# A routed feed-forward layer: the address of a tile's down weights found inside the next tile's up products, and the last 128 tokens handled some tiles later

## The chip, the cores and the metric

The kernel runs on one core of one Trainium2 chip. The metric is device time in microseconds (us) of one launch. The kernel before takes 870.91 us, the median of three runs (870.66 to 870.98). The compiler, the inputs and the launch are the same for both kernels.

## What is computed

A cross-attention layer is followed by a gated feed-forward layer with one shared expert and eight routed experts, of which each of the 2048 rows ("tokens": 8 batches of 256 rows, 512 numbers in each) takes two.

```python
x = x + xattn(layernorm(x), ctx, mask, ...)       # 8 batches, 16 heads
flat = layernorm(x).reshape(2048, 512)
shared = (sigmoid(flat @ shared_gate.T) * (flat @ shared_up.T)) @ shared_down.T
top_w, top_idx = top_k(softmax(flat @ router_w.T), 2)          # of 8 experts
ge, ue = einsum("nh,eih->nei", bf16(flat), w_gate), einsum(..., w_up)   # I = 352
de = einsum("nei,ehi->neh", sigmoid(ge) * ue, w_down)
out = layernorm(x) + x + shared + sum over experts of comb * de         # x: after attention
```

(The reference applies the layer to the normalised rows and adds the residual; the comment gives the sum in words.)

## The kernel before, in words

The program is written out by hand: every engine runs its instructions in the order in which the code issues them, and semaphores are put in from the reads and writes of tiles.

**Attention.** The loop over `b`, `g` and `h` (lines 1184 to 1262) runs the 8 batches. Beside it, the feed-forward work of the batch before is woven in by lists of steps: normalising rows (`token_norm`, line 530), turning them so that the hidden dimension lies on partitions (`turn_tokens`, line 547), choosing experts (`route`, line 564), and the shared expert (`shared_units`, line 928). Normalised rows are written to DRAM in `xs`, sorted by expert. Of the last batch, the first 128 rows are done in the loop; the last 128 rows are not sorted, and follow after it.

**Routed experts.** There are 37 tiles (`NT`) of 128 sorted rows, then 8 more tiles (`E`) in which the last 128 rows go through each of the 8 experts in turn. Which expert a sorted tile belongs to is known only at run time. Eight expert numbers are packed as base-8 digits of one integer, and TensorE's sequencer holds the integers in registers (`EIGHT`, line 797). `weights_of` (line 799) takes a tile's digit by a division and a remainder, multiplies it by the size of an expert's weights, and keeps the outcome in a register, `FIRST[t, per]`: once for a tile's gate and up weights (`GU`), once for its down weights (`DN`). It does so when it is first asked for a product's operand. The matmul's moving operand is then addressed by that register plus a constant.

**The order of the stage.** `stream` (line 858) lists the steps, and a round is named here by its tile number t. Round t holds `gate_up_of(t)`: eight products of 352 columns (four into `eg`, four into `eu`, line 820), then on ScalarE a tanh of `eg` (line 825), on VectorE the product `hz` (line 826), and on SyncE the fetch of tile t+3 (line 762). Then comes `down_of(t-2)`: three products of 512 columns into `ey` (line 849), a weighted copy by ScalarE (line 855), and a scatter to DRAM by GpSimd (line 856, recorded at line 195). Then `turn_h(t-1)`: three transposes of `hz` into `pht` (line 834) and their copy to `hT` (`evacuate`, line 95), which VectorE (line 98) and ScalarE (line 100) do in turn. The copy of an even tile is VectorE's, of an odd tile ScalarE's. So `down_of(t-2)` waits for ScalarE's copy in an odd round, for VectorE's in an even one.

**PSUM.** `bank` (line 80) gives out six banks in a ring; two of its six places draw on a pair of buffers with the tag "mm". A round takes four banks: `eg`, `eu`, `ey`, `pht`. `turn_tokens` (`pst`, line 552) and the router's products (`psr`, line 574) take an "mm" buffer directly, without a turn of the ring.

**Rounds and the last 128 tokens.** The code after the attention loop (lines 1264 to 1314) runs rounds 0 and 1, `token_norm` of the last 128 tokens on VectorE, round 2, `turn_tokens`, then rounds 3 to 37, with one of nine steps of `short` after each round from the fourth: eight of `route`, in which the router's products come first, and `weighted`, which makes eight diagonal matrices (line 873). None of these steps issues a DMA. Every third round one row block of the earlier result is read back (`again`, line 905, on GpSimd's queue). The turned rows `xTb`, the diagonals and `xT` are used from tile 37 on and by the shared expert that follows it.

Of the kernel before, what the change touches and what calls it, by code (L numbers as in the profile page):

```python
# [18 lines left out]
B, C, T = 8, 256, 512  # L19
HEADS, HD = 16, 16  # L20
E, I = 8, 352
NKC = T // P
# [10 lines left out]
NT = 2 * NS + E - 1  # L33
# [3 lines left out]
def xattn_ffn_kernel(  # L37
# [20 lines left out]
    nc = tc.nc  # L58
# [21 lines left out]
    def bank(shape, dt, name, own=False):  # L80


        ring.rotate(-1)
        i = 0 if own else ring[-1]
        if i == 0:
            return ps_m.tile(shape, dt, tag="long", name=name, bufs=1)
        if i in (3, 4):
            return ps_s.tile(shape, dt, tag=f"s{i - 2}", name=name)
        if i == 5:
            return ps_av.tile(shape, dt, tag="av", name=name)  # L90
        return ps_m.tile(shape, dt, tag="mm", name=name)
# [438 lines left out]
    def token_norm(b, tt, engine=nc.gpsimd):  # L530
        s = S[b]
        acc = s["acc", tt]
        mv, rs = s.pop(("tstats", tt))
        xn = one.tile([P, T], F32, tag="rd", name="xn")
        engine.tensor_scalar(xn, acc, mv[:, 0:1], rs, ALU.subtract, ALU.mult)
        engine.tensor_add(acc, acc, xn)
        s["xn", tt] = xn
# [3 lines left out]
    def late(tag, n=4):  # L541

        if tag not in LATE:
            LATE[tag] = one.tile([P, n, T], BF16, tag=tag, name="late_" + tag)
        return LATE[tag]

    def turn_tokens(b, tt):
        s = S[b]
        xn = s.pop(("xn", tt))
        if tt == 0:  # L550
            s["xT"] = two.tile([P, NKC, C], F32, tag="xT", name=f"xT{b}")
        ps = ps_m.tile([P, NKC, P], F32, tag="mm", name="pst")
        for kc in range(NKC):
            nc.tensor.transpose(ps[:, kc, :], xn[:, kc * P : (kc + 1) * P], ident)
        cols = slice(tt * P, (tt + 1) * P)
        nc.scalar.copy(s["xT"][:, :, cols], ps)
        if (b, tt) == (B - 1, 1):
            s["xTb"] = late("xm")[:, 0, :].rearrange("p (k n) -> p k n", n=P)
            nc.vector.tensor_copy(s["xTb"], ps)
        else:  # L560
            s["xnb", tt] = three.tile([P, T], BF16, tag="xnb", name="xnb")
            (nc.vector if b == B - 1 else nc.gpsimd).tensor_copy(s["xnb", tt], xn)
# [184 lines left out]
    def expert_tiles():  # L747
# [3 lines left out]
        ROW, EIGHT = [], []  # L751

        def fetch(t):

            if t >= NT:
                return
            if t == 0:
                ROW.extend(numbers(M["row"], THIRDS, mybir.EngineType.SP, P**3 - 1))
            v = ROW[t // 3]
            row = (v // P ** (t % 3)) % P * P if t % 3 else v % P * P  # L760
            XT[t] = late("ctx")[:, t % 4, :].rearrange("p (k n) -> p k n", n=P)
            nc.sync.dma_start_transpose(out=XT[t], in_=xs[bass.ds(row, P), :])
# [21 lines left out]
        GU, DN = (2 * NKC * I, flat(guT)), (3 * T, flat(dT))  # L784
        FIRST = {}
# [13 lines left out]
        def weights_of(t, W, n, at):  # L799


            per, cols = W
            if t >= NT:
                at += (t - NT) * per
                return cols[:, at : at + n]
            if (t, per) not in FIRST:
                v, i = EIGHT[t // 8], t % 8
                first = nc.tensor.to_reg(((v // 8**i) % 8 if i else v % 8) * per)
                FIRST[t, per] = nc.tensor.snap(
                    first, min_val=0, max_val=(E - 1) * per, guaranteed_mod_val=0, out_of_modulus=per  # L810
                )
            return cols[:, bass.ds(FIRST[t, per] + at, n)]

        def gate_up_of(t):
            xT = XT.pop(t) if t < NT else S[B - 1]["xTb"]
            pg = bank([P, I], F32, "eg")
            pu = bank([P, I], F32, "eu")
            for m, ps in ((0, pg), (1, pu)):
                for kc in range(NKC):
                    nc.tensor.matmul(  # L820
                        ps, xT[:, kc, :], weights_of(t, GU, I, (m * NKC + kc) * I),
                        start=(kc == 0), stop=(kc == NKC - 1),
                    )
            th = two.tile([P, I], F32, tag="th", name="eth")
            nc.scalar.activation(th, pg, AF.Tanh, scale=0.5)  # L825
            nc.vector.scalar_tensor_tensor(HZ[t % 2], th, 1.0, pu, ALU.add, ALU.mult)  # L826
            fetch(t + AHEAD)
# [15 lines left out]
        def down_of(t):  # L843
            ht = HT.pop(t)
            if t == NT:
                M["sum"] = bank([P, T], F32, "sum", True)
            ps = bank([P, T], F32, "ey") if t < NT else M["sum"]
            for ic in range(3):
                nc.tensor.matmul(  # L849
                    ps, ht[:, ic, :], weights_of(t, DN, T, ic * T),  # L850
                    start=(t <= NT and ic == 0), stop=(t < NT and ic == 2),
                )
            if t < NT:
                y = (late("mb", 2)[:, t % 5, :] if t % 5 < 2 else late("xm")[:, t % 5 - 1, :])
                nc.scalar.activation(y, ps, AF.Copy, scale=M["weight"][:, t : t + 1])
                scatter(zs, M["to"][:, t : t + 1], y, bounds_check=2 * ROWS - 1, oob_is_err=False)
# [21 lines left out]
    def give_back():  # L878


        halves = [(b, tt) for b in range(B) for tt in range(2)][:NS]
        room = deque(
            [four.tile([P, T], F32, tag=tag, name="again") for tag in "qk" for _ in range(3)]
        )
        for _ in range(3):
            e = three.tile([P, 2, T], F32, tag="e", name="again2")
            room.extend(e[:, i, :] for i in range(2))
        byrow = zs.rearrange("(r c) t -> r c t", c=2)
        Z = []

        def rooms(pool, tag, n, tiles=1):

            for _ in range(tiles):
                z = pool.tile([P, n, 2, T], BF16, tag=tag, name="z_" + tag)
                Z.extend(z[:, j] for j in range(n))

        def all_rooms():
            rooms(two, "V", 3, 2)
            rooms(three, "extra", 1, 3)
            rooms(two, "xT", 2)  # L900
            rooms(two, "x", 2)
            rooms(five, "acc", 1)
            rooms(one, "O", 1)

        def again(b, tt):
            S[b]["acc", tt] = a = room.popleft()
            nc.gpsimd.dma_start(out=a, in_=ACC[b][tt])

        def results(n):
            if not Z:  # L910
                all_rooms()
            nc.sync.dma_start(out=Z[n], in_=byrow[n * P : (n + 1) * P])

        def add(n, c):
            b, tt = halves[n]
            a = S[b]["acc", tt]
            nc.vector.tensor_add(a, a, Z[n][:, c, :])
            if c == 1:
                nc.sync.dma_start(out=out[b, tt * P : (tt + 1) * P, :], in_=a)

        n = range(NS)
        return (
            deque(lambda of=of: again(*of) for of in halves[: 2 * (NB - 1)]),
            deque(lambda i=i: results(i) for i in n), deque(lambda i=i, c=c: add(i, c) for i in n[:-1] for c in range(2)),
            lambda c: Z[NS - 1][:, c, :],
        )
# [257 lines left out]
    for b in range(B):  # L1184
# [10 lines left out]
        if 0 < b:  # L1195
            short = route(b - 1)
# [3 lines left out]
        elif b == B - 1:  # L1200
# [5 lines left out]
            fetch, whom, experts, weighted, tiles = expert_tiles()  # L1206
# [4 lines left out]
        for g in range(NG):  # L1211
            G = NG * b + g
            for h in range(8):
                st, half = divmod(h, 2)

                short = G == 0 and h < 6
# [49 lines left out]
    def some(todo, n):  # L1266
        for _ in range(min(n, len(todo))):
            todo.popleft()[1]()
# [10 lines left out]
    some(units, 3)  # L1279
    some(tiles, 3)  # L1280
    M["whom"]()
    token_norm(B - 1, 1, nc.vector)
    some(tiles, 3)
    turn_tokens(B - 1, 1)
    short = deque(route(B - 1, (1,)) + [(0.0, weighted)])
    again, results, adds, own_results = give_back()
    n = 2
    while n <= NT:
        some(tiles, 3)
        n += 1  # L1290
        if n >= 4:
            some(short, 1)
        if n % 3 == 0 and again:
            again.popleft()()
# [53 lines left out]
```

## Time and profile before

One profiled execution took 869.63 us: a span of 867.8 us from the first to the last instruction, and 1.83 us around it. The clock granted to TensorE was 1.00 throughout.

| what | value |
|---|---|
| median of three runs | 870.91 us |
| the profiled execution, its span | 869.63 us, 867.8 us |
| TensorE matmul busy in the span | 826.3 us (95%) |
| VectorE, ScalarE, GpSimd busy | 67%, 42%, 36% |
| rounds 0 to 4 of the expert stage | from 749.01 to 761.22 us |
| rounds 5 to 36 | from 761.22 to about 832.8 us |
| what follows, to the end | about 35 us |

Busy times are those of the engines proper; "PEld" is TensorE's weight load, which overlaps with its matmuls ("PE"). A name with a q behind it (PEldq) is an instruction of an engine's sequencer, such as the register arithmetic `FUSED_REGOPS`, and isn't counted as busy. In a row of a timeline the first two numbers are start and length in us, and a bracket gives idle time of the engine before it and what ended it. "issue" is time in which the engine waited for nothing that the profile shows. Matmuls are pipelined: a product of 352 columns is recorded with 0.31 us, but the next starts 0.149 us later; for one of 512 columns it is 0.38 us and 0.215 us.

### The profile page before, as it was taken

The numbers are of one execution on the slowest core, as the hardware profiler recorded it, in microseconds if no ns is written. First come the engines' busy times: TensorE is split into PE (matmuls) and PEld (weight loads), VectorE is DVE, ScalarE is ACT, GpSimd is POOL, SyncE is SP. The second block draws the span as 40 slices with busy tenths as digits, with TensorE's granted clock in tenths as the row PEclk, the third lists the DMA queues.
The fourth block names the chain that finished last, engine by engine and source line by source line (L and its number), as shares of the span: only waits on it lengthen the run. The fifth ranks groups of instructions, "written<-read, shape, count | busy, mean of one in ns | idle before, by whom it ended". The sixth has DMA issues, their size and how long they took to land.

```text
span 867.8 us, 13410 instructions
## 1 busy us (share of the span) xinstructions
PE 826.3 (95%) x4987; PEld 340.0 (39%) x4987; DVE 580.8 (67%) x1106; ACT 365.6 (42%) x478; POOL 312.6 (36%) x380
## 2 busy tenths in 40 slices
PE   7988989999999999999999999999999989899997
PEld 4322323333333334333433343433343333455573
DVE  7666767776777677867676778676766674543347
ACT  4234444343344334433443343434343445256632
POOL 3114303543354345343525151605251223155520
PEclk9999999999999999999999999999999999999999
DMA  4107962231551257115712350011000000267556
GB/s 159 46 33 239 342 192 78 34 45 43 128 100 30 41 123 122 23 36 123 128 22 42 90 99 1 26 34 52 1 25 13 13 13 25 61 147 170 150 169 242
DMA packets 91973, 75.05 MB, mean 86 GB/s; under 512 B 60321, under 2 KB 77756, under 8 KB 91526
## 3 DMA queue, kind: packets, MB, share of 16 engines
q1 hardware_dynamic: 85302, 53.84, 22.8%
q0 software_dynamic: 5904, 19.70, 10.8%
q8 instruction: 40, 0.66, 0.3%
q10 hardware_dynamic: 704, 0.66, 0.2%
q14 instruction: 23, 0.19, 0.1%
HBM read 37.84 MB, written 40.79 MB: 91 GB/s over the span
## 4 chain that ended last, share of the span: by engine, by line
PE 74%; DVE 19%; issue 3%; POOL 2%; ACT 1%; DMA 0%; DVEq 0%; ACTq 0%; POOLq 0%
PE s L436 24%; DVE nm L438 10%; PE av L474 9%; PE psy L998 5%; PE pu L940 4%; PE psq L411 3%; PE psk L411 3%; PE ey L849 3%; PE eu L820 3%; PE eg L820 3%; PE pgu L940 3%; PE pg L940 3%; DVE q L418 2%; PE s L459 2%; PE psv L378 2%
## 5 line engine op out<-in xcount | busy, mean ns | idle before, releaser
L461 ACT ACTIVATE e<-s 128x1024 f32<-128x1024 f32 x256 | 262.0, 1023 | 398.5 <-PE s L459 396.6
L438 DVE TENSOR_REDUCE nm<-s 128x2 f32<-128x1024 f32 x256 | 313.3, 1224 | 144.4 <-PE s L459 131.3
L436 PE MATMUL s<-k,q 32*128 32x512 f32 x1024 | 287.7, 639 | 25.3 <-DVE nm L438 22.7
L459 PE MATMUL s<-q,k 32*128 32x512 f32 x1024 | 288.5, 640 | 1.5 <-DVE q L448 0.8
L474 PE MATMUL av<-e,V 128*32 128x512 f32 x1024 | 137.4, 605 | 0.2 <-ACT e L461 0.2
L436 PEld LDWEIGHTS s<-k,q 32*128 32x128 f32 x1024 | 76.6, 183 | 130.2 <-DVE nm L438 104.7
L401 POOL TENSOR_SCALAR extra<-mb,alpha,beta 128x512 f32<-128x512 f32 x60 | 45.5, 763 | 146.1 <-DVE q L418 145.7
L343 POOL TENSOR_TENSOR rs<-ve,mhalf 128x1 f32<-128x1 f32 x32 | 18.4, 575 | 217.0 <-DVE ve L341 216.9
L459 PEld LDWEIGHTS s<-q,k 32*128 32x128 f32 x1024 | 76.5, 182 | 5.3 <-issue 4.3
L474 PEld LDWEIGHTS av<-e,V 128*32 128x32 f32 x1024 | 20.3, 108 | 98.2 <-issue 96.3
L195 POOL DMA_INDIRECT xs<-xnb,at x30 | 30.2, 1006 | 73.9 <-DVE at L669 59.3
L826 DVE SCALAR_TENSOR_TENSOR hz<-eth,eu 128x352 bf16<-128x352 f32 x45 | 23.4, 520 | 41.6 <-ACT eth L825 18.2
L998 PE MATMUL psy<-sdT,h 128*128 128x512 f32 (+1 forms) x90 | 45.3, 615 | 0.2 <-issue 0.2
L940 PE MATMUL pu<-xT,sguT 128*128 128x256 f32 x128 | 36.7, 403 | 0.0
L940 PE MATMUL pg<-xT,sguT 128*128 128x256 f32 x128 | 35.3, 401 | 0.0
L378 PE MATMUL psv<-WvT,ctx 128*128 128x256 f32 x128 | 34.8, 394 | 0.0
L940 PE MATMUL pgu<-xT,sguT 128*96 128x256 f32 (+1 forms) x128 | 34.1, 393 | 0.0
L820 PEld LDWEIGHTS <-late_ctx 128*128 128x128 bf16 x296 | 27.6, 98 | 14.0 <-issue 2.6
L411 PE MATMUL psq<-xm,WqT 128*128 128x512 f32 x64 | 32.0, 620 | 0.9 <-DVE xm L1103 0.9
L195 POOL DMA_INDIRECT whose<-who,at x30 | 29.0, 968 | 9.1 <-issue 9.1
L940 PEld LDWEIGHTS pu<-xT,sguT 128*128 128x128 f32 x128 | 21.8, 189 | 25.3 <-issue 22.8
L411 PE MATMUL psk<-ctx,WkT 128*128 128x512 f32 x64 | 31.6, 617 | 0.0
(219 smaller groups left out, 980.4 us busy)
## 6 DMA issues: line engine op xcount, KB each, us to landing
xs<-blank SPq DMA_DIRECT2D x7, 1920.0 KB
x<-in_x_dram SPq DMA_DIRECT2D x7, 512.0 KB
ctx<-in_ctx_dram SPq DMA_DIRECT2D x7, 512.0 KB
accd<-acc SPq DMA_DIRECT2D x12, 256.0 KB
again<-accd POOLq DMA_DIRECT2D x12, 256.0 KB
out_dram<-again SPq DMA_DIRECT2D x12, 256.0 KB
gu<-in_L_ffn_w_gate_dram POOLq DMA_DIRECT2D x8, 352.0 KB
gu<-in_L_ffn_w_up_dram POOLq DMA_DIRECT2D x8, 352.0 KB
```

Source lines behind the costliest of these rows:

```text
L195: i = nc.gpsimd.indirect_dma_start(to[:, :], bass.IndirectOffsetOnAxis(ap=rows, axis=0), what, None, **bounds).ins
L378: nc.tensor.matmul(ps, ct[:, kc, sc * P : (sc + 1) * P], WvT[:, kc, :], start=(kc == 0), stop=(kc == 1))
L401: engine.tensor_scalar(t, S[b]["mb"], at, be, ALU.mult, ALU.add)
L411: nc.tensor.matmul(ps, W[:, kc, g // 2].rearrange("p j a d -> p (j a d)"), rhs[:, kc, :], start=(kc == 0), stop=(kc == 1),)
L436: nc.tensor.matmul(ps[:, jj, :], q[r, tci * P : (tci + 1) * P], k[r, :], start=True, stop=True)
L438: best = lambda: nc.vector.reduce_max(NM[G % 2][:, tci, c0 : c0 + 33 : 32], ps, axis=AX.X)
L459: nc.tensor.matmul(ps[:, jj, :], k[r, sc * P : (sc + 1) * P], q[r, :], start=True, stop=True)
L461: nc.scalar.activation(e, ps, AF.Exp)
L474: nc.tensor.matmul(AVT[G][32 * j : 32 * j + 32, :], V[:, sc, 2 * g + j // 2, j % 2 : j % 2 + 2, :].rearrange("p o d -> p (o d)"), et[j // ...
L820: nc.tensor.matmul(ps, xT[:, kc, :], weights_of(t, GU, I, (m * NKC + kc) * I), start=(kc == 0), stop=(kc == NKC - 1),)
L940: lambda kc=kc: nc.tensor.matmul(ps, sguT[:, m, kc, i0 : i0 + n + more], s["xT"][:, kc, :], start=(kc == 0), stop=(kc == NKC - 1))
L998: nc.tensor.matmul(t["y"], t["h"][:n, ic, tt * P : (tt + 1) * P], sdT[:n, ic, :], start=(ic == 0 and b < B - 1), stop=(ic == 2),)
```

## The change

The arithmetic of the register is moved into a function of its own, `find`, which `weights_of` still calls where a register isn't there yet. In `gate_up_of(t)`, for t from 1 to 37, `find(t - 1, DN[0])` is called just ahead of the eighth product. `down_of(t - 1)`, which runs a round later, then has its register already. The address for the gate and up weights is found where it was.

The last 128 tokens: `token_norm` moves from behind round 1 to behind round 6, `turn_tokens` from behind round 2 to behind round 8, and the nine steps of `short` from the ends of rounds 4 to 12 to those of rounds 10 to 18. `give_back`, which sets aside tiles and issues nothing, is now called before them.

```diff
             if (t, per) not in FIRST:
-                v, i = EIGHT[t // 8], t % 8
-                first = nc.tensor.to_reg(((v // 8**i) % 8 if i else v % 8) * per)
-                FIRST[t, per] = nc.tensor.snap(
-                    first, min_val=0, max_val=(E - 1) * per, guaranteed_mod_val=0, out_of_modulus=per
-                )
+                find(t, per)
             return cols[:, bass.ds(FIRST[t, per] + at, n)]
+
+        def find(t, per):
+
+            v, i = EIGHT[t // 8], t % 8
+            first = nc.tensor.to_reg(((v // 8**i) % 8 if i else v % 8) * per)
+            FIRST[t, per] = nc.tensor.snap(
+                first, min_val=0, max_val=(E - 1) * per, guaranteed_mod_val=0, out_of_modulus=per
+            )
...
                 for kc in range(NKC):
+                    if (m, kc) == (1, NKC - 1) and 0 < t <= NT:
+                        find(t - 1, DN[0])
                     nc.tensor.matmul(
...
     M["whom"]()
-    token_norm(B - 1, 1, nc.vector)
     some(tiles, 3)
-    turn_tokens(B - 1, 1)
-    short = deque(route(B - 1, (1,)) + [(0.0, weighted)])
     again, results, adds, own_results = give_back()
     n = 2
     while n <= NT:
         some(tiles, 3)
         n += 1
-        if n >= 4:
+
+        if n == 6:
+            token_norm(B - 1, 1, nc.vector)
+        elif n == 8:
+            turn_tokens(B - 1, 1)
+            short = deque(route(B - 1, (1,)) + [(0.0, weighted)])
+        elif n > 9:
             some(short, 1)
```

## The prediction

> **What bounds the kernel now.** I read the page first, then the chain that ended last, then TensorE's timeline by round, then the register instructions of its sequencer.
>
> ```profile
> PE 826.3 (95%) x4987; PEld 340.0 (39%) x4987; DVE 580.8 (67%) x1106; ACT 365.6 (42%) x478; POOL 312.6 (36%) x380
> ```
>
> TensorE is the bound nearly everywhere, and the change touches only the expert stage. There the chain of waits runs along TensorE too, so only gaps between its products can be won. A round of eight products at 0.149 us, three at 0.215 and three transposes at 0.055 needs 2.00 us. The timeline of the rounds shows which ones take longer:
>
> ```profile
> 789.06 0.76 PE L820 MATMUL eu<-guT,late_ctx 128*128 x4
> 789.65 0.81 PE L849 MATMUL ey<-dT,hT 128*128 x3
> 791.07 0.76 PE L820 MATMUL eu<-guT,late_ctx 128*128 x4
> 791.88 0.81 PE L849 MATMUL ey<-dT,hT 128*128 x3
> ```
>
> In the first pair (an even round, t=18) the down products start 0.60 us after the first up product, that is four times 0.149: no gap. In the second (t=19) they start 0.82 us after it: 0.22 us are lost. Over the whole stage the even rounds lose nothing. Of the odd ones, t=7 to 37, four (9, 17, 25, 33) lose 0.15 us each and twelve lose 0.21 to 0.22: 3.18 us in all. Round 3 loses 0.06, round 5 nothing.
>
> ```profile
> 790.50 0.69 ACT L855 ACTIVATE late_mb<-ey,weight 128x512 bf16<-128x512 f32 x1 [0.78 <-issue]
> 791.09 0.47 ACT L100 COPY hT<-pht 128x384 bf16<-128x384 bf16 x1
> ```
>
> ```profile
> L808 PEldq FUSED_REGOPS  x1: 232/232/232, 791.6 to 791.6; - x1
> ```
>
> ```profile
> 790.92 0.55 PEld L820 LDWEIGHTS <-late_ctx 128*128 128x128 bf16 x4
> 791.61 0.10 PEld L849 LDWEIGHTS <-hT 128*128 128x128 bf16 x1
> ```
>
> In an odd round `hT` comes from ScalarE behind the copy of `ey`, and ends at 791.56, 0.05 us after the last up product began (791.513). The load of `hT` starts at 791.61, in every one of the 16 rounds 0.095 us after the last up product's start. The address arithmetic (L808) starts with it, at 0.090, takes 0.16 us (in the four rounds, whose down tiles 7, 15, 23 and 31 are the top digits of their integers) or 0.22 to 0.23, and the product follows 0.05 us after its end: 0.09 + 0.23 + 0.05 = 0.37, against a pitch of 0.149. This fits all 16 within 0.003 us. So the gap is not the wait for `hT`; it is the arithmetic that can't start until that wait is over. In even rounds `hT` is early, and the arithmetic runs 0.2 to 0.4 us ahead of the products.
>
> **The address.** The change has `find`'s division, remainder and multiplication done in the round before, ahead of the eighth product. What stays ahead of the first down product is the step from the register to a byte address. Its nearest rows are the same steps of the other products:
>
> ```profile
> L849 PEldq FUSED_REGOPS  x74: 46/46/46, 753.0 to 831.6; - x74
> ```
>
> The product then starts 0.090 + 0.046 + 0.050 = 0.186 us after the last up product, 0.037 late. Bounds: nothing left (the first product might need no step of its own, and without register work the load and the product start together, as below), or 0.07, if the step takes half as long again.
>
> ```profile
> 857.73 0.60 PE L849 MATMUL sum<-dT,hT 128*128 128x512 bf16 x2 [0.62 <-ACT hT L841]
> 857.73 0.33 PEld L849 LDWEIGHTS <-hT 128*128 128x128 bf16 x3 [0.80 <-ACT hT L841]
> ```
>
> I take 0.037. A rule speaks against there being anything to win: by the Trainium skill ("Perfetto Trace Analysis", section "Per-engine timelines", its TensorE part) the sequencer pushes a load or product into a wait queue and goes on to the next instruction before the semaphores are satisfied. Then the arithmetic would run during the wait, and the move would give 0. The rows decide otherwise: 16 times of 16 it starts within 0.006 us of the load that waited. By the rule the sum is 0, by the rows 3.18 less the rest.
>
> What hides the arithmetic where it goes? It delays the eighth product by up to 0.23 us of the sequencer's time. In odd rounds that product's own step ends 0.62 us before it starts. In even ones the lead is 0.25 to 0.45; I get that from the start of L808 (0.22 to 0.44 ahead of the last up product) and the 0.124 us between two such steps. With 0.23 more ahead of it, the tightest even round keeps some 0.02. The sequencer does the same work in all, so later rounds are not short of it. If every lead were 0.02 smaller, one round would be late by under 0.01; I put nothing, and keep the other end for rival 5. Behind the moved instruction stand the eighth product, its readers (`hz` on VectorE, idle 0.9 us ahead of it) and nothing of SyncE or GpSimd. A register is held one round longer; that adds no instruction.
>
> Once an odd round is shorter, what is late next? ScalarE's chain to `hT` starts from the previous `ey`, so the load stays at 0.095. VectorE's `hT` for the even round ends near 789.02, 0.48 us ahead of its load. ScalarE works 1.6 us of a round, GpSimd's scatter 0.99. They keep pace.
>
> **The last 128 tokens.** This moves work without removing any. TensorE: four transposes (0.44 us) and eight router products (0.91). ScalarE: one copy of 0.60 and an exponential of 0.21. VectorE: 0.54 + 0.69 for the norm, 0.69 for `xTb`, about twenty steps of 0.15 to 0.20, eight diagonals of 0.25; GpSimd 0.61. No DMA. It passes SyncE's fetches and GpSimd's scatters and read-backs of about six rounds, which share only engine time with it. What it costs where it is:
>
> ```profile
> 754.10 0.69 ACT late_mb L855
> 754.79 0.37 ACT hT L100
> 755.16 0.12 ACT xT L556
> 755.27 0.25 issue
> 755.52 0.49 ACT eth L825
> 756.02 0.04 issue
> 756.06 0.76 PE eu L820 x4
> ...
> 758.89 0.67 issue
> 759.57 0.70 ACT late_xm L855
> 760.26 0.04 issue
> 760.30 1.06 PE psr L581 x8
> ```
>
> In round 3 the up products wait 1.00 us for the tanh of the same round's `eg`: the transposes have taken one of the two "mm" buffers, so both halves come to lie in the other one. Behind round 4 the router's products wait 0.77 us for the copy of the `ey` just made. With the products themselves this is 3.12 us in rounds 3 to 5. Moved by six rounds, it meets the ring of six banks in the same phase (24 banks, four turns), and the same parity of ScalarE and VectorE. So the waits return. The first shrinks to about 0.96: ScalarE's copy of `ey` starts 0.03 us after the round's first TensorE instruction there, instead of 0.08. The saving is 0.04 to 0.05. The norm falls into VectorE's idle time of 1.5 us between an even round's `hz` and the next one's. Bounds: if the other buffer is given, the `eu` wait ends with VectorE's copy of the transposes (756.37 instead of 756.01) and the router's with ScalarE's `hT` (760.62 instead of 760.25), 0.73 more; if both waits vanish, 1.77 less.
>
> The odd rounds' gaps change places: 3 and 5 now have theirs, 9 and 11 lose theirs in the new waits. Round 3's is 0.08, since ScalarE's copy, and so `hT`, is 0.05 later there.
>
> **Sum.** Out: 3.18 + 0.06. In: 15 rounds of 0.037 and one of 0.08, 0.64. The move: -0.05. Together -2.65. The stage after shifts as a whole, since its DMAs start from the last scatter. On the profiled execution that is 869.63 - 2.65 = 866.98. It lay 1.28 under the median, so for the median 870.91 - 2.65 = 868.26.
>
> **Rivals.** (1) The register work is still placed behind the wait, so that the change doesn't do what it says, or the queue behaves as the rule has it: 870.9. Against it: the program's order, and that even rounds already run it early. (2) The PSUM waits don't return in the steady rounds: 868.26 - 1.77 = 866.5. Against it: `ey` and `pht` are fresh behind any round of that phase. (3) They return longer: 868.6 to 869.0. (4) The early rounds were held by something else that the waits cover (the first fetches, the first copy), so that what leaves isn't won and what arrives is paid: up to 868.26 + 3.1 = 871.4. Fetches run three tiles ahead without a wait there, which speaks against it. (5) Slower: in each of the 18 even rounds the eighth product waits for its sequencer, because it isn't ahead of TensorE as I read it. With no lead at all it pays 0.23, and 0.046 if its own step then comes as an instruction apart: 18 x 0.276 = 5.0 us, 873.3. It decides from a lead under 0.23 us, and eats up my gain at 0.15 us a round, a lead of about 0.13; the least that I read is 0.25.
>
> **How the numbers follow.** A measurement of this kernel tells about 0.2% (1.74 us) from no change. Forecast as summed, 867.6 to 869.0: 0.64. (1) 0.08, (2) 0.07, (3) 0.10, (4) 0.06, (5) 0.05. Faster by over 0.2% (under 869.17): the forecast and (2) nearly whole and most of (3), 0.77. Slower by over 0.2% (above 872.65): (5) and 0.01 for what I don't see, 0.06. The rest is 0.17. The range 866.8 to 871.0 takes in the forecast, (1), (3) and a part of (2) and (4), and leaves out under 2 in 10.
>
> **What would show it.** In the profile after, odd rounds should have 0.63 us from the first up to the first down product, not 0.82, with L808 ahead of the last up product. Even rounds stay at 0.60. The transposes `pst` should stand ahead of round 9's products, with about 1 us ahead of its `eu` and 0.8 ahead of `psr` behind round 10; rounds 3 to 5 should run at 2.0 us. I am wrong if odd rounds keep 0.75 to 0.82, if a gap opens ahead of an eighth product, or if rounds 0 to 5 don't shorten by 3.

## The result, and the profile after

The changed kernel takes 868.17 us, the median of 7 runs (866.56 to 869.80); the kernel before, beside it on the same chip, takes 870.98 (869.33 to 872.91, 7 runs). The ratio is 0.997, with a 95% interval of 0.9958 to 0.9982. The forecast was 868.26.

Single runs scatter by more than the parts of the change are worth, so the comparison of traces is made on the **stage**: the time from the first `eg` product to the end of the program, in one profiled execution each. It is 118.81 us before (749.01 to 867.82) and 116.15 after (750.25 to 866.39): 2.67 us less. TensorE's work is the same; the page's first line hardly moves.

The page of the changed kernel, busy us by engine:

```profile
PE 826.5 (95%) x4987; PEld 341.0 (39%) x4987; DVE 580.7 (67%) x1106; ACT 365.9 (42%) x478; POOL 313.6 (36%) x380
```

The timeline of the changed kernel over the same two rounds as before, t=18 and t=19 (start, length, engine, line; the up products are now line 826, the down products line 855):

```profile
789.32 0.76 PE L826 MATMUL eu<-guT,late_ctx 128*128 x4
...
789.91 0.81 PE L855 MATMUL ey<-dT,hT 128*128 x3
...
791.33 0.76 PE L826 MATMUL eu<-guT,late_ctx 128*128 x4
791.35 0.47 ACT L100 COPY hT<-pht 128x384 bf16<-128x384 bf16 x1
...
791.87 0.40 PEld L855 LDWEIGHTS <-hT 128*128 128x128 bf16 x3
791.96 0.81 PE L855 MATMUL ey<-dT,hT 128*128 x3
```

In the odd round, t=19, ScalarE's copy ends at 791.82, again 0.05 us after the last up product began (791.774), and the load starts 0.097 us after that product's start (before 0.095). But the first down product now starts 0.63 us after the first up product, not 0.82. The even round keeps its 0.59 to 0.60. The arithmetic that stood in that gap has moved ahead. This is line 813 of the changed kernel within that odd round's up products:

```profile
L813 PEldq FUSED_REGOPS  x1: 227/227/227, 791.1 to 791.1; - x1
```

It starts 0.66 us ahead of the last up product and takes the same 0.23 us. What is left behind the wait is the step to the byte address, 0.042 us, the shorter of the two in this row (791.6 to 792.0):

```profile
L855 PEldq FUSED_REGOPS  x2: 42/44/46, 791.9 to 792.0; - x2
```

The chain that ended last, of the changed kernel, around rounds 9 and 10, where the last 128 tokens now fall:

```profile
767.61 0.46 PE pst L554 x4
...
768.71 0.20 issue
768.90 0.50 ACT eth L831
769.40 0.04 issue
769.44 0.79 PE eu L826 x4
...
772.25 0.67 issue
772.92 0.70 ACT late_xm L861
773.62 0.04 issue
773.66 1.06 PE psr L581 x8
```

The two waits that rounds 3 and 4 had are back in the same shape, in round 9 and behind round 10: `eu` waits 0.96 us for the tanh of the same round, `psr` 0.775 for the copy of the `ey` just made. Rounds 2, 3 and 4 have shrunk from 2.46, 3.06 and 3.70 us to 2.02, 2.09 and 2.01; rounds 8, 9 and 10 have grown to 2.45, 2.99 and 3.70.

### The profile page after: what moved, and what is told of

Same layout as the page of the kernel before. It is cut to its first block, busy times and chain, and to the rows that moved or that the text cites. A ratio compares the mean times of both kernels' runs of the same rounds, so it can differ in the third digit from the quotient of the medians.

```text
span 866.4 us, 13437 instructions
## 1 busy us (share of the span) xinstructions
PE 826.5 (95%) x4987; PEld 341.0 (39%) x4987; DVE 580.7 (67%) x1106; ACT 365.9 (42%) x478; POOL 313.6 (36%) x380
## 4 chain that ended last, share of the span: by engine, by line
PE 75%; DVE 19%; issue 3%; POOL 2%; ACT 1%; DMA 0%; DVEq 0%; ACTq 0%; POOLq 0%
PE s L436 24%; DVE nm L438 10%; PE av L474 9%; PE psy L1004 5%; PE pu L946 4%; PE psq L411 4%; PE psk L411 3%; PE eu L826 3%; PE eg L826 3%; PE ey L855 3%; PE pgu L946 3%; PE pg L946 3%; DVE q L418 2%; PE s L459 2%; PE psv L378 2%
```

## The experiments

Each is measured twice: by its median beside the kernel before (ratio with interval), and by the stage of its profiled execution, against 118.81 us before and 116.15 after. Lengths of rounds run from the first `eg` product to the next round's. (So counted, rounds 5 to 36 of the kernel before end at 828.40, and 39.4 us follow; the 832.8 of the table above is about where the down products of the last sorted tile end.)

**1. The address alone.** The changed kernel, with the last 128 tokens at their old place.

```diff
+    token_norm(B - 1, 1, nc.vector)
     some(tiles, 3)
+    turn_tokens(B - 1, 1)
+    short = deque(route(B - 1, (1,)) + [(0.0, weighted)])
...
-        if n == 6:
-            token_norm(B - 1, 1, nc.vector)
-        elif n == 8:
-            turn_tokens(B - 1, 1)
-            short = deque(route(B - 1, (1,)) + [(0.0, weighted)])
-        elif n > 9:
+        if n >= 4:
```

> The changed kernel with the last 128 tokens put back where they were, so that only the early address is left. Theory (the gaps of the odd rounds are the address arithmetic that waits behind the load of hT): odd rounds lose 0.033 us instead of 0.15 to 0.22, rounds 3 to 5 keep their waits of 1.00 and 0.77; 2.6 us under the kernel before, 868.3. Rival (the gain comes from taking the last 128 tokens out of the crowded first rounds): within 0.5 of the kernel before.

Measured: 868.75 us (22 runs), ratio 0.9975 (0.9966 to 0.9984); stage 116.29. Odd rounds from the seventh on take 2.04 us, where before they took 2.15 to 2.23. Rounds t=18 and t=19 of this kernel:

```profile
789.12 0.76 PE L826 MATMUL eu<-guT,late_ctx 128*128 x4
789.71 0.81 PE L855 MATMUL ey<-dT,hT 128*128 x3
...
791.12 0.76 PE L826 MATMUL eu<-guT,late_ctx 128*128 x4
791.75 0.81 PE L855 MATMUL ey<-dT,hT 128*128 x3
```

Rounds 2 and 3 are 0.05 and 0.09 longer than before. In round 3 the eighth product starts 0.148 us late: the sequencer, held by the wait ahead of `eu`, has its steps and `find` to do behind it. So 2.52 of the 2.67 us come from the address; most of the other 0.15 is this late product, which shrinks to 0.032 in round 9 of the changed kernel.

**2. The last 128 tokens alone.** The kernel before, with the other half of the diff: the move of `token_norm`, `turn_tokens` and `short` to `n == 6`, `n == 8` and `n > 9`.

> The kernel before with only the last 128 tokens moved. Theory: their waits move to rounds 9 and 10 with 0.95 and 0.77 us, the odd rounds keep 0.15 to 0.22; 0.05 us under the kernel before, 870.9. Rival (the gain comes from the tokens): 2 to 3 us under it, 868.2.

Measured: 871.13 us (14 runs), ratio 1.0002 (0.999 to 1.0013); stage 118.87. Odd rounds keep their 2.15 to 2.23 us; rounds 8, 9 and 10 take 2.45, 3.01 and 3.70. The chain shows `eu` of round 9 behind the tanh, and the copy of `ey` ahead of the router's products:

```profile
771.87 0.49 ACT eth L825
772.37 0.04 issue
772.41 0.76 PE eu L820 x4
...
775.91 0.70 ACT late_xm L855
```

Rounds 2 to 4 become 2.92 us shorter in all, rounds 8 to 10 2.99 longer: the move only changes where this is paid.

**3. The copy of `hT` early, the address late.** The kernel before, in `turn_h`: here it is not the arithmetic that moves, but the wait ahead of it.

```diff
-                evacuate(HT[t], ps)
+                nc.vector.tensor_copy(HT[t], ps)
```

> The kernel before, address as it was, with hT copied by VectorE in every round, so that it is early in odd rounds too. Theory (arithmetic is exposed only behind a load that waits): with no late hT the sequencer does the address ahead and all odd gaps go, though the address is found where it was; 3.2 us less, and up to 0.4 more in round 3, where ScalarE has one copy less ahead of its tanh: 867.4. Rival (the arithmetic delays the product wherever it stands): the odd rounds still lose 0.15 us or more, 870 to 871.

Measured: 867.40 us (11 runs), ratio 0.9965 (0.9953 to 0.9976); stage 115.30. All steady rounds take 2.008 us. In the timeline of this kernel the odd round t=19 (the second pair) looks like the even one ahead of it, 0.59 us from the first up to the first down product, with the late address still in its place:

```profile
788.33 0.76 PE L820 MATMUL eu<-guT,late_ctx 128*128 x4
788.93 0.81 PE L849 MATMUL ey<-dT,hT 128*128 x3
...
790.34 0.76 PE L820 MATMUL eu<-guT,late_ctx 128*128 x4
790.93 0.81 PE L849 MATMUL ey<-dT,hT 128*128 x3
```

Once VectorE makes `hT` in every round (0.36 us, from 0.22 us after the transposes), it is there before TensorE's sequencer comes to the load. Then the sequencer isn't held, and runs the arithmetic ahead of the products: in the odd rounds from the seventh on it ends mostly 0.35 to 0.43 us ahead of the first down product (0.26 at the least), in the kernel before 0.05. The gap needs both: an operand that comes late, and arithmetic placed behind it. The stage falls by 3.51: 3.12 in the lengths of the odd rounds from the seventh on, 0.39 in rounds 3 and 4, where ScalarE had this copy to make as well.

**4. The tokens at another place.** The changed kernel, with `token_norm` and the transposes one round later and the router's products two.

```diff
-        if n == 6:
+        if n == 7:
...
-        elif n == 8:
+        elif n == 9:
...
-        elif n > 9:
+        elif n > 11:
```

> The changed kernel with the last 128 tokens' turn behind round 9 and the router's products behind round 12, where neither of the two mm buffers is wanted by the next round's first products. Theory (their waits are a matter of the ring's phase): the waits of 0.96 and 0.77 us go, rounds 9 and 11 get the odd rounds' 0.033 back; 1.66 us under the changed kernel, 866.5. Rival (they come from ScalarE's and VectorE's extra work wherever it stands): both waits stay, 868.2.

Measured: 867.23 us (10 runs), ratio to the kernel before 0.9962 (0.995 to 0.9973); stage 114.43, which is 1.72 less than the changed kernel's. The chain of this kernel around the transposes:

```profile
768.55 0.44 PE pst L554 x4
769.00 0.60 PE eg L826 x4
769.59 0.60 PE eu L826 x4
```

`eu` follows `eg` without a wait, as it should where the turn of the ring gives the two halves different buffers (this was worked out from the code, not read in the trace). The waits of 0.96 and 0.775 sum to 1.73, and this is what goes. So they hang on the place where the work meets the ring of banks, and not on the transposes or the router as such.

**5. The arithmetic made longer, late.** The kernel before, with two needless divisions in the address of the down weights. They leave the address as it is, since (3e+1)/3 is e without its remainder.

```diff
-                first = nc.tensor.to_reg(((v // 8**i) % 8 if i else v % 8) * per)
+                e = (v // 8**i) % 8 if i else v % 8
+                if per == DN[0]:
+                    for _ in range(2):
+                        e = nc.tensor.snap(nc.tensor.to_reg(e * 3 + 1), min_val=1, max_val=22) // 3
+                first = nc.tensor.to_reg(e * per)
```

> The kernel before with two needless divisions in the arithmetic of the down address, at its old place; the value stays the same. Theory (in odd rounds all of that arithmetic lies between the load of hT and the first down product): each odd round from 7 to 37 loses about 0.2 us more, 16 x 0.2 = 3.2; even rounds, which are ahead by 0.14 to 0.36, lose 0.05 at most, 0.3 in all; 874.3. Rival (the odd rounds lose by ScalarE's late copy and not by the arithmetic): no more than 0.5 over the kernel before.

Measured: 880.33 us (4 runs), ratio 1.0106 (1.0085 to 1.0127); stage 127.26, 8.45 more. Odd rounds from the thirteenth on take 2.56 us on average instead of 2.20, even ones 2.16 instead of 2.01. The direction is right, the size was missed: the two divisions don't take 0.2 us but 0.36 in twelve of the odd rounds and 0.30 in the other four. In round 19 one instruction of 0.23 us has become three, of 0.27, 0.20 and 0.03, with 0.06 between them:

```profile
L811 PEldq FUSED_REGOPS  x2: 195/232/268, 795.2 to 795.5; - x2
L853 PEldq ALU_OP  x1: 32/32/32, 795.8 to 795.8; - x1
```

That is so much that even rounds, whose copy comes early, no longer hide the arithmetic.

**6. The arithmetic made longer, early.** The same two divisions in the changed kernel's `find`.

> The changed kernel with the same two divisions in find, ahead of the eighth product. Theory (the sequencer's lead over the eighth product covers find, with 0.1 to 0.3 us to spare in most even rounds and more in odd ones): odd rounds as before; the tightest even rounds get up to 0.13 us late at the eighth product, 0.5 us in all, 868.7. Rival 5 of the prediction (the lead is nearly used up by find as it is): each even round loses most of the 0.2, 3 to 4 us, 872.

Measured: 873.87 us (20 runs), ratio to the kernel before 1.0029 (1.0022 to 1.0036); stage 122.20, 6.06 more than the changed kernel's. My expectation failed. The down products' gaps are nearly gone, and a new one has opened in the timeline of this kernel:

```profile
789.14 0.83 PE L830 MATMUL eu<-guT,late_ctx 128*128 x4
789.81 0.81 PE L859 MATMUL ey<-dT,hT 128*128 x3
...
791.22 0.91 PE L830 MATMUL eu<-guT,late_ctx 128*128 x4
791.97 0.81 PE L859 MATMUL ey<-dT,hT 128*128 x3
```

Four up products at their pitch take 0.76 us. Here they take 0.83 and 0.91: the eighth product starts late by 0.07 and 0.15, in an odd round too. Over all rounds that makes 6.48 us, 0.34 of it in round 1. Two readings were open: TensorE's sequencer has so much to do in a round that what is added no longer fits; or any addition ahead of the eighth product is paid, because nothing is spare there. Runs 9 and 10 were made to tell them apart.

**7 and 8. Everything that helps, and the same without the early address.** Run 7 is run 4 with run 3's line; run 8 is run 7 with the address back in its late place.

> The changed kernel with the last 128 tokens in the other phase of the ring (turn behind round 9, router behind round 12) and hT copied by VectorE in every round. Theory: what is left of the odd gaps goes too; the stage takes 113.9 us instead of 114.4 with the other phase alone and 118.8 in the kernel before; 866.1. Rival (VectorE's extra copies delay hz or hT): even or odd rounds over 2.01 us, no better than 867.2.

> The same with the address found where it was in the kernel before. Theory (early address and early hT are two ways to the same gap): within 0.15 us of the kernel with all three in the stage, 866.1. Rival (the early address is worth something by itself): 2 us or more over it, 868.

Measured: 865.93 us (5 runs), ratio to the kernel before 0.9932 (0.9918 to 0.9945), stage 113.84; and 865.96 us (5 runs), 0.9936 (0.9922 to 0.9949), stage 113.81. In both, rounds from the third on without the tokens' work take 2.008 us. The early address adds nothing once `hT` is early. The two are ways to the same gap, and the copy by VectorE closes all of it.

**9 and 10. One division, late and early.** As runs 5 and 6, with `range(1)`.

> The kernel before, with one needless division (of 3e+1 by 3) put into the finding of each down address, in its late place. It adds a multiplication with addition and a division as an instruction of the sequencer, by half of what two of them added late: 0.18 us in each odd round. Both theories expect the 16 odd rounds to lose it whole, 16 x 0.18 = 2.9 us, and the even ones up to 0.5 us in all: stage 118.81 + 2.9 to 3.4 = 121.7 to 122.2 us, the time some 3 us over the kernel before. What this run settles is the added instruction's own duration.

> The changed kernel with the same one division, in the early place. Theory (what TensorE's sequencer does in a round, in all, must fit into the round; with nothing added it has about 0.28 us of a round's 2.01 us free): 0.18 us more fits, so few eighth products are late, the rounds stay at 2.01 to 2.04 us, and the stage is 116.15 + 0 to 0.6 = 116.2 to 116.8 us. Rival (only the lead ahead of the eighth product counts, and it is used up by what the change already put there): each even round, at least, loses most of 0.18 us, and the stage is 116.15 + 18 x 0.15 = 118.9 us or more. Linear between the changed kernel and the one with two divisions early would be 116.15 + 3.0 = 119.2.

Measured, late: 875.00 us (15 runs), ratio 1.0049 (1.0037 to 1.0062); stage 122.69, 3.88 more. Odd rounds take 0.20 us longer. 0.33 of the 3.88 lies behind round 37, where `pht` waits 0.4 us for VectorE, which is adding up rows read back; in rounds 0 to 37 it is 3.56.

Measured, early: 869.69 us (20 runs), ratio to the kernel before 0.998 (0.997 to 0.999); stage 117.89, 1.75 more than the changed kernel's. 0.69 of it is that same wait of `pht`, here 0.8 us; why it is longer stays open. In rounds 0 to 37 it is 1.06. With the wait the stage lies midway between the two expectations; without it, at 117.20, nearer to the first. The sequencer's rows within the rounds (count, and shortest, median and longest in ns) give the reason. The changed kernel, the arithmetic and a short step of the up products (`ALU_OP`):

```profile
L813 PEldq FUSED_REGOPS  x63: 158/222/232, 760.9 to 826.6; - x63
L826 PEldq ALU_OP  x19: 32/32/32, 775.1 to 823.8; - x19
```

One division early, its first instruction, and the second one of round 20:

```profile
L816 PEldq FUSED_REGOPS  x33: 227/258/268, 760.1 to 827.5; - x33
L817 PEldq FUSED_REGOPS  x1: 125/125/125, 794.3 to 794.3; - x1
```

What counts is the least time from the start of `find` to the eighth product. In the changed kernel it is 0.22 to 0.23 us for `find`, 0.058 of pause, 0.032 for the product's own address step, and 0.029 to the product: 0.35 us. (The 0.029 is read in round 3 of run 1, where the product is late.) In two rounds of eight, where the tile's digit is the lowest or the top one of its integer, the step is part of `find`, and it is 0.23, as in round 9. With one division it is an instruction of 0.26, 0.06 of pause, a second of 0.125 and 0.05 to the product: 0.50, or 0.28 in the two rounds of eight. So the division adds 0.15 or 0.05, 0.13 on average; the second one adds another 0.20 on average (0.67 and 0.58 in run 6).

Measured against that least time, the changed kernel's even rounds have 0.01 to 0.35 us to spare, 0.15 on average over 16 (4 to 36, without 12). With one division more, 11 of 18 even rounds start the eighth product at just the limit, late by up to 0.13 us. Steady rounds (12 to 35) take 2.044 us on average instead of 2.023; with two divisions they take 2.178, 0.155 longer.

So the spare time is real, about 0.15 us of a round: the first 0.13 us a round costs 1.06 in all, the next 0.20 costs 5.01. Late, the steps are 3.56 and 4.84. The second reading, that all is paid, would have given 18 x 0.13 = 2.3 us or more early for the first division.

## Why the prediction was right

**The gap is the arithmetic behind the wait.** Runs 1, 3 and 8 show it from both sides: moving either the arithmetic or the copy removes it, and run 2, which moves neither, keeps it. Runs 5 and 9 lengthen it as the arithmetic is lengthened. Rival 1 falls, and in this case the rule weighed there, that the sequencer goes on while an instruction waits: in the kernel before it went on in none of the 16 odd rounds, and only taking the wait or the arithmetic away helped. Nor did it go on while `eu` waited in round 3 of the kernel before. From 754.4 to 756.1 line 820 has this one row:

```profile
L820 PEldq FUSED_REGOPS  x1: 46/46/46, 756.1 to 756.1; - x1
```

It starts at 756.054, 0.005 us ahead of the product that waited. Whether the waiting instruction itself holds the sequencer or a queue that is full behind it, no run tells apart.

**The step that stays.** I took 0.037 us for each odd round; it is 0.033, since the step takes 0.042 us and not 0.046. The odd gaps sum to 0.58 us (15 rounds of 0.033, 0.081 in round 3), where I had 0.64. Round 3's own 0.08 came out as put.

**The tokens' move.** I expected that the waits return, at 0.96 and 0.77; they did, at 0.956 and 0.775. In the changed kernel the gaps give -2.62 of the -2.67, and the rest is about the -0.05 that I put; taken singly the move is worth +0.06 without the early address (run 2) and -0.15 with it (run 1). Rivals 2 to 4 fall: no wait vanished, none is longer, and rounds 2 to 4 did run at 2.0 to 2.1. But rival 2 was closer than its chance of 0.07 says: one round further on, the 1.72 us it spoke of are there to be had (run 4).

**The eighth product.** My reading, that after the change the tightest even round keeps 0.02 us, was about right: round 20 keeps 0.01. The only late one was in an odd round, 9, behind the tokens' wait, by 0.032 us. So rival 5 falls. But what I put beside it, that the sequencer's work stays the same in all, is wrong: the step ahead of the first down product now stands apart, and in six rounds of eight so does the eighth product's own, as rival 5 had allowed. In rounds 18 and 19 the sequencer has 24 register instructions, 1.80 us in all, where the kernel before has 22 and 1.68. That this cost nothing is owed to the spare time, and I had not seen how little is left: runs 6 and 10 show that rival 5's mechanism exists and decides from about 0.15 us more work in a round.

**The sum.** -2.65 against -2.67 in the stage; in the medians 870.98 to 868.17, -2.81. The two whole profiled executions differ by only 1.46 us (869.63 and 868.17). The stage of the changed kernel began 1.24 us later, at 750.25 instead of 749.01, which is about the 1.28 by which the execution of before lay under its median. Between its 200th and 300th matmul (49 to 68 us) it fell 1.63 us behind; the next section shows what lies there.

## What to carry to other kernels

Where an engine's sequencer has to work out an address, ask what it is queued behind: here arithmetic behind an instruction that waits cost nearly its whole length, and the same arithmetic ahead of it cost nothing as long as the sequencer's work of a round fitted into the round. Before moving the arithmetic, ask whether the awaited operand could come earlier: here one line, the copy by an engine with idle time, was worth more than the change. And where a piece of work taken from a ring of buffers causes a wait, try it one step further along the ring before moving it far away.

## What was not expected of the hardware

**Half-clock stretches in mid-program.** The rows of the stretch from 40 to 60 us (busy time of each engine, granted clock, DMA share, GB/s), of the kernel before and the changed kernel:

```profile
40.00:60.00 20.00, 17.05 (x111) 5.71 (x103) 12.63 (x15) 7.24 (x8) 0.11 (x1) 1.00 0.13 47
```

```profile
40.00:60.00 20.00, 17.37 (x99) 5.53 (x95) 11.79 (x15) 6.01 (x7) 0.00 (x0) 0.91 0.10 26
```

In the second, one stretch of 3.41 us, beginning at 51.75, runs at half the clock, though TensorE is as busy as in the first; fewer matmuls (99 for 111) get done. The change touches nothing there, and in the 3.41 us just ahead of it TensorE is busy for 2.31 us in either kernel. Seven of the twelve profiled executions of this case have one such stretch, beginning between 33 and 53 us; what sets it off no run here shows. Of 44 timed runs of the kernel before, the 16 with a mean clock of 1.000 have a median of 869.7 us, the 10 with 0.998 one of 871.2 (a stretch of 3.41 us at half clock lowers the mean by 0.002; that these runs had one is inferred). That is more than half of what the change was worth, and a reason why a stage, not a span, was compared. It is not the only source of scatter: in runs 2, 7 and 8 TensorE once stands idle for 1.36 or 1.37 us ahead of a product of line 436, at full clock, and no run shows why.

**The sequencer as a resource.** TensorE's sequencer spends 0.85 us of a 2.02-us round on between eleven and twelve register instructions (rounds 12 to 35 of the changed kernel), most of them 0.046 us long with 0.078 us to the next. The pause between two such instructions is now and then 0.1 to 0.23 us, about once in a round; no run shows why. In rounds 14 and 20 of run 10, which are late by 0.13, one of 0.23 stands ahead of the eighth product.
